# Attention's SBUF arithmetic on another engine, a denser mixing schedule, and a third-batch second layer in products of eighths

## The chip, the cores and the metric

The kernel runs on one core of one Trainium2 chip. The metric is device time in microseconds (us). Engines are named as in the profile: PE (matmul), PEld (PE's weight loads), DVE (vector), ACT (scalar), POOL (GpSimd), SP (the queue that issues every DMA here).

## The reference, cut to what matters

Everything is float32, on x of 4 batches by 2048 tokens by 512 features. A local attention (16 heads of 32, windows of 128 tokens, each window looking at itself and its two neighbours) stands between two layer norms; then comes a feed-forward part whose weights are blended anew for each batch:

```python
x = x + layernorm(attention(layernorm(x), w_qkv))
xn = layernorm(x)
h = relu(xn @ gate_w1.T + gate_b1)
g = mean over tokens of (h @ gate_w2.T + gate_b2)      # 8 numbers per batch
mW1 = W1 + sum_e g[e] * TW1[e]                         # 2048 x 512
mW2 = W2 + sum_e g[e] * TW2[e]                         # 512 x 2048
u = gelu(xn @ mW1.T + mb1)
out = x + layernorm(u @ mW2.T + mb2)
```

## The kernel before, in words

Work is laid out by hand: each engine executes its instructions in the order in which the program text issues them (`manual_schedule`), so a line's place in the text is its place in its engine's queue. There are two stages.

**Attention.** 256 slots, `i = 0..255` (loop at L962): slot `i` is window `i // 4` and head group `i % 4`. In a slot PE computes the scores of slot `i + 1` (L649), turns the probabilities of slot `i` (L686), does up to eight matmuls of "dense" work (products of the QKV projection or of the gate, L518) and the values (L707). DVE takes the row maxima of the next slot's scores (L658), ACT the exponentials (L671) and the copies of the turned probabilities (L691). Lists named `mid`, `rest`, `late` and so on hold what is done at certain points of a slot. `residual` (L326) and `normed` (L334) finish a window after its output: normalise, add the input, store the sum to DRAM, take its statistics, normalise again; the result is turned by PE (`xn2_transposes`, L338) one slot after `normed`. `norm_tile` (L435) normalises an input tile. The dense products follow the Strassen-Winograd scheme of seven products of quarter matrices; `right_factors` (L474) makes the sums T1 to T4 of the right operand, two operations in each of two slots. All of that arithmetic is on DVE. POOL does only the tiny steps of the statistics (L96, L98).

**Blending.** `mixer()` (L106) is a generator. A step loads one expert's 512 KB piece and adds it, scaled, to an accumulator on DVE (L155); after eight experts four quarter sums follow (L163 to L166) and the piece is stored to DRAM in the form that the seven products need. 512 experts in all. `MIXED` (L961) says how many steps each of 16 slots takes: 22 in 16, from slot 85 on; the four quarter sums count as a step. The rest is done in the feed-forward stage by `mixing(...)` between products. Loads run three steps ahead, in four buffers.

**Feed forward.** 16 blocks of 512 tokens (`for K in range(NBK)`, L1485), four blocks to a batch. A block has a first layer (four sets of seven products, L1023, with one `step()` after the other in `middle`) and a second layer. For blocks 0 to 11 that is `second` (L1157): seven products of quarter matrices, each of 16 matmuls of 128x256. For the last batch, blocks 12 to 15, it is `second_deep` (L1237): each of the seven products (index `o`) is again done as seven (`inner(0)` to `inner(6)`, L1308, four matmuls of 128x128 each), so 49 small products. Its right-hand sums are made on DVE as it goes (`inner_sums`, L1233), the results are added on DVE (L1270, by `add` and `emit`), and its weights need a further set of sums, made beforehand by `inner_mixer` (L174): 14 steps of load, four DVE additions and store. Before, that runs in block 11's second layer and block 12's first. At `o == 2` four POOL operations (L1344) turn T1 into T4, which the last product (`o == 6`) reads. At `o == 6` the statistics of two output rows are taken (L1354) before the addition that follows `inner(4)`.

Of the kernel before, what the change touches and what calls it, by code (L numbers as in the profile page):

```python
# [9 lines left out]
F32 = mybir.dt.float32  # L10
# [6 lines left out]
P = 128  # L17
# [17 lines left out]
def sandwich(ctx: ExitStack, tc: tile.TileContext, x, w_qkv, gw1, gb1, gw2, gb2, w1, b1, w2, b2, tw1, tb1, tw2, tb2, out):  # L35
# [44 lines left out]
    DEEP = (NB - 1,)  # L80
# [20 lines left out]
    def normalize(dst, src, sm):  # L101
        mv, rs = sm
        nc.vector.tensor_scalar(dst, src, mv[:, 0:1], rs, ALU.subtract, ALU.mult)


    def mixer():  # L106

        todo = [(b, s, c, e) for b in range(NB) for s in range(2) for c in range(HC) for e in range(NX)]
# [6 lines left out]
        def load(n):  # L115
            b, s, c, e = todo[n]
# [31 lines left out]
        for n, (b, s, c, e) in enumerate(todo):  # L148
# [4 lines left out]
            late = []  # L153
            acc = accs[b, s, c]
            nc.vector.scalar_tensor_tensor(acc, ets.pop(n), g_all[b][:, e : e + 1], acc, ALU.mult, ALU.add)  # L155
            yield
            if e == NX - 1:
# [5 lines left out]
                nc.vector.tensor_tensor(sums[:, 0, :], a21, a22, ALU.add)  # L163
                nc.vector.tensor_tensor(a21, a11, a21, ALU.subtract)
                nc.vector.tensor_tensor(sums[:, 1, :], sums[:, 0, :], a11, ALU.subtract)
                nc.vector.tensor_tensor(sums[:, 2, :], a12, sums[:, 1, :], ALU.subtract)  # L166
                late.append(lambda b=b, s=s, c=c, acc=acc, sums=sums: store(b, s, c, acc, sums))
                yield
        for f in late:
            f()  # L170

    issued = {b: 0 for b in DEEP}

    def inner_mixer(b):  # L174

        todo = [(o, h) for o in order_deep for h in range(2)]
        loaded, late = {}, []

        def load(n):
            o, h = todo[n]  # L180
            two = slice(2 * h, 2 * h + 2)
            et = mix.tile([P, 4, 2, P], F32, tag="exps", bufs=4, name=f"inner_{b}_{o}_{h}")
            nc.sync.dma_start(et[:, :2], m3_d[b][:, o, 0:8:7, two, :])
            nc.sync.dma_start(et[:, 2:], m3_d[b][:, o, 3:7:3, two, :])
            loaded[n] = et

        def store(n, et):
            o, h = todo[n]
            two = slice(2 * h, 2 * h + 2)
            nc.sync.dma_start(m3_d[b][:, o, 1, two, :], et[:, 3])  # L190
            nc.sync.dma_start(m3_d[b][:, o, 2, two, :], et[:, 0])
            nc.sync.dma_start(m3_d[b][:, o, 4:6, two, :], et[:, 1:3])
            issued[b] = n + 1

        for n in range(2):
            load(n)
        yield
        for n in range(len(todo)):
            for f in late:
                f()  # L200
            if n + 2 < len(todo):
                load(n + 2)
            et = loaded.pop(n)
            f11, f21, f12, f22 = (et[:, i] for i in range(4))
            nc.vector.tensor_tensor(f22, f21, f22, ALU.add)
            nc.vector.tensor_tensor(f21, f11, f21, ALU.subtract)
            nc.vector.tensor_tensor(f11, f22, f11, ALU.subtract)
            nc.vector.tensor_tensor(f12, f12, f11, ALU.subtract)
            late = [lambda n=n, et=et: store(n, et)]
            yield  # L210
        for f in late:
            f()
# [48 lines left out]
    def gate_end(b, hsum, bank, spare):  # L261
# [24 lines left out]

        def first_biases():
# [38 lines left out]
    def residual(W_):  # L326
        st = win[W_]
        x1 = st["x1"]
        normalize(x1, st["a"], st["sb"])
        nc.vector.tensor_tensor(x1, x1, st["x"], ALU.add)  # L330
        nc.sync.dma_start(x1_d[W_], x1)
        st["sc"] = stats(x1, f"c{W_}")

    def normed(W_):  # L334
        st = win[W_]
        normalize(st["xn2"], st["x1"], st["sc"])
# [1268 lines left out]
```

## Time and profile before

| what | value |
|---|---|
| median of 3 runs | 3224.7 us (3222.76 to 3225.04) |
| the profiled execution, its own time | 3224.83 us |
| its span, first to last instruction | 3223.0 us |
| granted PE clock | 0.998 |
| PE busy | 3197.1 us (99%) |
| DVE busy | 2278.8 us (71%) |
| ACT busy | 1576.5 us (49%) |
| POOL busy | 676.5 us (21%) |
| attention stage | 0 to about 1674 us |
| blending in the attention stage | from about 589 us |
| feed forward | about 1674 us to the end |

The span is 1.8 us shorter than the time of the same execution. A matmul in float32 stands in the profile as two records, so a product of 16 matmuls is counted x32. A "wait" is idle time of an engine that ended with another's signal. A timeline's first two columns are the start and the duration in us.

### The profile page before, as it was taken

To read this page: it belongs to the slowest core of one execution; us is meant where nothing else is said; L and a number is where in the kernel's file an instruction comes from. 1 tells how busy PE (TensorE), PEld (TensorE's weight loads), DVE (VectorE), ACT (ScalarE), POOL (GpSimd) and SP (SyncE) were. 2 spreads that over 40 slices of the span, in tenths; PEclk is the share of its full clock that TensorE was granted. 3 is DMA by queue.
4 is the path that set the end of the run, shared out by engine and by line. 5 is a ranking of instruction groups with operands and counts; after the bars stand their busy time and mean duration, and the time that the engine had idled before them with its cause. 6 is when DMAs were issued, how large, how long until landed. Compare 5 with 4: busy or idle time off the path is not lost.

```text
span 3223.0 us, 61653 instructions
## 1 busy us (share of the span) xinstructions
PE 3197.1 (99%) x23862; PEld 2697.0 (84%) x23862; DVE 2278.8 (71%) x3307; ACT 1576.5 (49%) x4332; POOL 676.5 (21%) x847
## 2 busy tenths in 40 slices
PE   9999999999999999999999999999999999999998
PEld 7788888888788888878768888888888888889998
DVE  5766666888998889888865665677657667554555
ACT  3777777777777777777761222112222112222222
POOL 0111111111111111110112322323322323332233
PEclk9999999999999999999999999999999999999999
DMA  2111112455555556554677889999899999874555
GB/s 87 54 57 54 40 60 80 138 189 163 193 193 168 178 177 200 194 174 151 211 277 277 310 309 345 355 337 330 311 330 361 341 326 322 305 246 155 193 187 170
DMA packets 363334, 688.88 MB, mean 214 GB/s; under 512 B 27161, under 2 KB 115353, under 8 KB 357026
## 3 DMA queue, kind: packets, MB, share of 16 engines
q1 hardware_dynamic: 363042, 684.94, 61.4%
q8 instruction: 189, 3.10, 0.4%
q14 instruction: 103, 0.84, 0.1%
HBM read 567.39 MB, written 117.44 MB: 212 GB/s over the span
## 4 chain that ended last, share of the span: by engine, by line
PE 94%; DVE 2%; DMA 2%; ACT 1%; POOL 0%; issue 0%; SPq 0%; POOLq 0%; DVEq 0%; ACTq 0%
PE pm L518 23%; PE px L1023 13%; PE ptp L686 11%; PE px L1143 7%; PE sc L649 7%; PE pz L1023 6%; PE po L707 5%; PE pz L1143 5%; PE py L1023 3%; PE py L1143 3%; PE px L1308 2%; PE py2b L1143 2%; PE pz L1308 1%; PE pm L582 1%; PE ptx L340 1%; PE pto L311 1%
## 5 line engine op out<-in xcount | busy, mean ns | idle before, releaser
L155 DVE SCALAR_TENSOR_TENSOR acc<-exps,g,acc 128x1024 f32<-128x1024 f32 x512 | 697.1, 1362 | 66.1 <-DMA exps<-in_tw 60.1
L658 DVE TENSOR_REDUCE nm<-sc 128x2 f32<-128x768 f32 (+1 forms) x512 | 449.2, 918 | 206.8 <-PE sc L649 201.8
L671 ACT ACTIVATE pr<-sc,nm 128x384 f32<-128x384 f32 (+1 forms) x1024 | 572.8, 592 | 11.3 <-DVE nm L658 11.1
L691 ACT COPY prT<-ptp 128x512 f32<-128x512 f32 x732 | 382.9, 595 | 281.3 <-PE ptp L686 281.1
L686 PEld LDWEIGHTS ptp<-ident,pr 128*128 128x128 f32 x2944 | 318.0, 141 | 102.3 <-issue 89.8
L686 PE MATMUL ptp<-ident,pr 128*128 128x128 f32 x2944 | 378.7, 278 | 0.0
L1060 ACT COPY py<-px 128x512 f32<-128x512 f32 x63 | 36.0, 571 | 662.6 <-PE px L1023 662.4
L1023 PE MATMUL px<-tT,w 128*128 128x256 f32 x1512 | 350.1, 379 | 0.6 <-DVE cpv L1083 0.6
L1023 PEld LDWEIGHTS px<-tT,w 128*128 128x128 f32 x1512 | 286.9, 190 | 40.0 <-DVE cpv L1083 1.0
L649 PE MATMUL sc<-k,q 32*128 32x384 f32 (+2 forms) x2816 | 243.2, 423 | 3.7 <-ACT pr L671 3.5
L671 ACT ACTIVATION_READ_ACCUMULATOR pr<-sc,nm 128x1 f32 x1024 | 236.5, 231 | 0.0
L1080 DVE TENSOR_TENSOR cpb<-pz,cpb 128x512 f32<-128x512 f32 x63 | 43.4, 689 | 268.8 <-PE pz L1023 240.1
L96 POOL TENSOR_SCALAR ve_b<-mv_b 128x1 f32<-128x1 f32 x64 | 42.8, 669 | 819.2 <-DVE mv_b L94 819.2
L707 PEld LDWEIGHTS po<-prT,v 128*32 128x32 f32 x5888 | 152.2, 110 | 50.9 <-ACT pr L671 25.4
L707 PE MATMUL po<-prT,v 128*32 128x128 f32 x5888 | 189.7, 275 | 0.2
L649 PEld LDWEIGHTS sc<-k,q 32*128 32x128 f32 x2816 | 118.7, 184 | 74.4 <-issue 53.9
L1143 PE MATMUL px<-w2s,u 128*128 128x256 f32 x784 | 175.1, 379 | 0.0
L518 PE MATMUL pm<-xnT,wqkv 128*128 128x256 f32 x720 | 172.2, 382 | 0.0
L1105 POOL TENSOR_TENSOR t<-u 128x512 f32<-128x512 f32 x60 | 79.9, 1332 | 434.8 <-ACT u L1035 434.8
L1143 PEld LDWEIGHTS px<-w2s,u 128*128 128x128 f32 x784 | 149.0, 190 | 20.2
L518 PEld LDWEIGHTS pm<-xnT,wqkv 128*128 128x128 f32 x720 | 132.0, 190 | 16.7
L1074 ACT COPY cpb<-px 128x512 f32<-128x512 f32 x63 | 36.9, 585 | 182.0 <-PE px L1023 182.0
(295 smaller groups left out, 5911.6 us busy)
## 6 DMA issues: line engine op xcount, KB each, us to landing
exps<-in_tw SPq DMA_DIRECT2D x512, 512.0 KB, 6.0
w2s<-m2d SPq DMA_DIRECT2D x168, 512.0 KB, 8.1
w2s<-m3d SPq DMA_DIRECT2D x84, 512.0 KB, 4.7
acc<-in_w SPq DMA_DIRECT2D x64, 512.0 KB, 6.1
x<-in_x SPq DMA_DIRECT2D x64, 256.0 KB, 4.2
m1d<-acc SPq DMA_DIRECT2D x64, 256.0 KB, 6.3
w<-m1d SPq DMA_DIRECT2D x16, 1024.0 KB, 7.9
fxT<-xTd SPq DMA_DIRECT2D x16, 1024.0 KB, 8.5
```

The source lines that it names most:

```text
L155: nc.vector.scalar_tensor_tensor(acc, ets.pop(n), g_all[b][:, e : e + 1], acc, ALU.mult, ALU.add)
L518: nc.tensor.matmul(bank[u not in chain][:, half, :], lhsT=a[:, kc, ts(half, P)], rhs=b[:, kc, :], start=(u not in (2, 3, 4) and half == kc ...
L649: nc.tensor.matmul(scs[r // 2][:, r % 2, col : col + nj * W], lhsT=q[rows, g, ts(W_ % WB, W)], rhs=k_of[kb][rows, g, j0 * W : (j0 + nj) * ...
L658: nc.vector.tensor_reduce(st["nm"][:, h : h + 2], scs[u][:, :, : nk * W], AX.X, ALU.max, negate=True)
L671: nc.scalar.activation(pr[:, : nk * W], scs[r // 2][:, r % 2, : nk * W], AF.Exp, bias=st["nm"][:, h : h + 1], accum_out=st["den"][:, h : h ...
L686: nc.tensor.transpose(pt[:, r, :], st["pr"][g * 4 + r][:, ts(j, W)], ident)
L691: nc.scalar.copy(prT, pt)
L707: nc.tensor.matmul(po[r * E : (r + 1) * E, n, :], lhsT=v_of[kb][:, jj, h * E : (h + 1) * E], rhs=prT[:, r, :], start=(j == 0), stop=(j == ...
L1023: nc.tensor.matmul(bank[:, f, :], lhsT=factor[:, f, kc * P : (kc + 1) * P], rhs=right[:, kc, :], start=(start and f == 0 and kc == 0), sto ...
L1105: nc.gpsimd.tensor_tensor(t1s[c], b12, us[c][:, :, :Q], ALU.subtract)
L1143: nc.tensor.matmul(bank[:, t, :], lhsT=right(c - c % 2)[:, c % 2, ts(t, P)], rhs=w[:, c % (HC // 2), :], start=(start and c == 0 and t == ...
L1308: nc.tensor.matmul(bank, lhsT=right(p), rhs=w[:, p, :], start=(start and p == 0), stop=True, skip_group_check=True,)
```

## The change

- In the attention loop the arithmetic that reads and writes SBUF alone moves from DVE to POOL: `residual`'s normalise and add, `normed`, `norm_tile` from the third block on, `right_factors` from the second block on, and the blending's four quarter sums (which are then no step of their own). The last window, in the feed-forward stage, and the prologue keep DVE.
- `residual` is split. Its store to DRAM and its statistics become `residual_stats`, at the end of the slot.
- `MIXED` goes from 22 steps in 16 slots to 29; the third step of a slot stands after the first reading of the dense product.
- Batch 2 is added to the batches whose second layer is done in 49 small products. The 14 inner weight sums of batch 2 are put between the steps of batch 3's blending, one after each piece but the first; those of batch 3 now run as the only steps of block 8's first layer. By then all blending is done.
- In `second_deep` the four POOL operations of T4 are issued as two at `o == 3` and two at `o == 4`, and at `o == 6` the addition after `inner(4)` (with the next of the waiting DVE sums) comes before the row statistics, not after them.

```diff
-    DEEP = (NB - 1,)
+    DEEP = (NB - 2, NB - 1)
...
-    def normalize(dst, src, sm):
+    def normalize(dst, src, sm, engine=nc.vector):
         mv, rs = sm
-        nc.vector.tensor_scalar(dst, src, mv[:, 0:1], rs, ALU.subtract, ALU.mult)
+        engine.tensor_scalar(dst, src, mv[:, 0:1], rs, ALU.subtract, ALU.mult)
...
-        todo = [(b, s, c, e) for b in range(NB) for s in range(2) for c in range(HC) for e in range(NX)]
+        todo = []
+        for b in range(NB):
+            again = [(b - 1, o, h) for o in order_deep for h in range(2)] if b - 1 in DEEP else []
+            for s in range(2):
+                for c in range(HC):
+                    todo += [(b, s, c, e) for e in range(NX)]
+                    if s or c:
+                        todo += again[:1]
+                        del again[:1]
...
+            if len(what) == 3:
+                et = ets.pop(n)
+                sum_inner(et)
+                late.append(lambda what=what, et=et: store_inner(*what, et))
+                yield
+                continue
...
-                nc.vector.tensor_tensor(sums[:, 0, :], a21, a22, ALU.add)
+                engine = nc.gpsimd if attending[0] else nc.vector
+                engine.tensor_tensor(sums[:, 0, :], a21, a22, ALU.add)
...
-    def residual(W_):
+    def residual(W_, engine=nc.gpsimd):
         st = win[W_]
         x1 = st["x1"]
-        normalize(x1, st["a"], st["sb"])
-        nc.vector.tensor_tensor(x1, x1, st["x"], ALU.add)
-        nc.sync.dma_start(x1_d[W_], x1)
-        st["sc"] = stats(x1, f"c{W_}")
+        normalize(x1, st["a"], st["sb"], engine)
+        engine.tensor_tensor(x1, x1, st["x"], ALU.add)
+
+    def residual_stats(W_):
+        st = win[W_]
+        nc.sync.dma_start(x1_d[W_], st["x1"])
+        st["sc"] = stats(st["x1"], f"c{W_}")
...
-        def right_factors(K, part, i=0):
+        def right_factors(K, part, i=0, engine=nc.gpsimd):
...
             rest[i + 1].append(lambda W_=W_: residual(W_))
+            late[i + 1].append(lambda W_=W_: residual_stats(W_))
             rest[i + 2].append(lambda W_=W_: normed(W_))
...
-        MIXED = (1, 0, 1, 1, 2, 1, 1, 2, 2, 1, 1, 1, 2, 1, 2, 2)
+        MIXED = (2, 1, 1, 3, 2, 1, 1, 3, 2, 1, 1, 3, 2, 2, 1, 3)
...
-                if o == 2:
-                    for p in range(PAIRS2):
+                if o in (3, 4):
+                    for p in range(2 * o - 6, 2 * o - 4):
                         nc.gpsimd.tensor_tensor(t1[:, p], bottom[:, p, :, :Q], t2[p // 2][:, p % 2], ALU.subtract)
...
+                inner(4, X, summed(2))
+                add(r[1, 1], X, r[1, 1])
+                run(dve, 1)
                 if o == 6:
                     row1 = [stats(y[1][:, t, :], f"d{K}_{t + 2}") for t in range(2)]
...
-                inner(4, X, summed(2))
-                add(r[1, 1], X, r[1, 1])
-                run(dve, 1)
...
-                if K // NBLK in DEEP and k == 0:
+                if b == DEEP[0] and k == 0:
+                    if c == 0:
+                        assert next(blend, 0) == 0
+                        inner = inner_mixer(NB - 1)
                     step = lambda: next(inner, None)
```

## The prediction

> **What bounds the kernel now.** I read first the page's busy times and the chain of work that ended last:
>
> ```profile
> PE 3197.1 (99%) x23862; PEld 2697.0 (84%) x23862; DVE 2278.8 (71%) x3307; ACT 1576.5 (49%) x4332; POOL 676.5 (21%) x847
> ...
> PE 94%; DVE 2%; DMA 2%; ACT 1%; POOL 0%; issue 0%; SPq 0%; POOLq 0%; DVEq 0%; ACTq 0%
> ```
>
> PE is the path. Only three things move the end: less PE work, PE waits that go, PE waits that come. The second view is busy time by stage, for 16 attention slots with blending and 16 without:
>
> ```profile
> 638.96:742.83 103.87, 103.87 (x1041) 84.62 (x1042) 92.08 (x132) 77.33 (x224) 13.54 (x24) 1.00 0.56 186
> ...
> 229.38:333.25 103.87, 103.87 (x1041) 84.62 (x1042) 66.44 (x105) 77.31 (x224) 11.61 (x24) 1.00 0.17 53
> ```
>
> The columns are length, PE, PEld, DVE, ACT, POOL, clock, DMA share, GB/s. DVE goes from 66 to 92 of 103.87 us and PE takes the same 103.87 us. So the attention stage has nothing to win from a lighter DVE, and the list of PE's waits agrees: between 540 and 1100 us it is empty.
>
> The third view is PE's timeline in a block of batch 3 (block 13), at the end of product 2 and of product 6:
>
> ```profile
> 2996.73 1.06 PE L1308 MATMUL pz<-w2s,u 128*128 128x128 f32 x8
> 2998.61 1.16 PE L1308 MATMUL px<-w2s,inner_right 128*128 128x128 f32 x8 [0.82 <-DVE y L1270]
> ...
> 3022.83 1.06 PE L1308 MATMUL pz<-w2s,t 128*128 128x128 f32 x8
> 3024.27 1.16 PE L1308 MATMUL px<-w2s,inner_right 128*128 128x128 f32 x8 [0.39 <-DVE y L1270]
> 3025.26 1.89 PE L1023 MATMUL px<-fxT,w 128*128 128x256 f32 x8
> ```
>
> Small products follow each other every 0.893 us, but these starts lie 1.88 and 1.44 us apart: 0.98 and 0.55 us lost. Both wait for a DVE addition (the one after `inner(4)`), so the fourth view is DVE and POOL there:
>
> ```profile
> 2991.85 1.47 DVE L1233 TENSOR_TENSOR inner_right<-u,inner_right 128x512 f32<-128x512 f32 x1
> ...
> 2996.80 1.55 DVE L1233 TENSOR_TENSOR inner_right<-u,inner_right 128x512 f32<-128x512 f32 x1
> 2998.27 0.28 DVE L1270 TENSOR_TENSOR y<-px,y 128x128 f32<-128x128 f32 x1
> ...
> 3009.84 0.68 DVE L1233 TENSOR_TENSOR inner_right<-u,inner_right 128x512 f32<-128x512 f32 x1
> ...
> 3022.34 0.69 DVE L92 BATCH_NORM_STATS2 st_d<-y 128x6 f32<-128x512 f32 x1
> ...
> 3023.95 0.26 DVE L1270 TENSOR_TENSOR y<-px,y 128x128 f32<-128x128 f32 x1
> ```
> ```profile
> 2990.94 6.86 POOL L1344 TENSOR_TENSOR t<-u,t 128x512 f32<-128x512 f32 x4 [6.14 <-PE pz L1308]
> ```
>
> In product 2, DVE's sums take 1.47 and 1.55 us in place of 0.68 while POOL makes T4, and the addition comes late. In product 6 the two statistics (1.6 us) stand ahead of the addition.
>
> **The second layer of blocks 8 to 11.** Blocks begin at 2739.48 and 2836.17 us (block 11, seven products): 96.69 us. Blocks 13 and 14 begin at 2931.25 and 3025.26, and 15 at 3119.27: 94.01 us each. The difference is 2.68 us, times four blocks: **-10.7 us**. The working agrees: 7 x 6.907 = 48.35 us of PE becomes 49 x 0.893 = 43.76, 4.59 less, of which 1.53 goes back in the two waits and about 0.4 in the hand-overs between the layers. The added POOL, ACT and DVE work of these blocks is what blocks 13 and 14 carry within their 94.01 us; blending is gone from there by then, so DVE's busy time falls from 68 us (block 9) to the 46 of block 13, and the DMA share from 0.92 to 0.49.
>
> **The addition before the statistics.** PE's fifth small product ends at about 3022.8, so the addition can start at about 3023.0 and be done before PE needs it at 3023.7. The 0.55 us go in blocks 8 to 14: 7 x 0.55 = **-3.85 us**. Later on DVE are then the statistics, by 0.9 us; nothing on PE waits for those. In block 15 the end is DVE's own chain, from 3209.69: there the addition must wait some 0.7 us for PE with nothing ahead of it, so the statistics and all after them shift: **+0.7 us**.
>
> **T4 summed later.** The four POOL operations wait for PE to have read T1 in product 1 (the row above says so: released by PE's `pz`, at 2990.94 us). POOL has no other work between there and product 5, so an issue further down the text starts at the same moment and meets the same DVE sums. **0 us**; bounds 0 and -0.98 x 8 = -7.8 us, if something of products 3 and 4 did hold it.
>
> **Entry into block 8.** Block 12, the first deep one before, took 2836.17 to 2931.25 = 95.08 us, 1.07 more than 13: its right-hand sums started 0.3 us later and met POOL twice (the chain shows `inner_right` there). Block 8 gets this too; block 12 keeps it. Besides, all 14 inner sums now stand in block 8's first layer, 16 steps in 48 us, 3.0 us each: a step has 1.7 us of DVE and hangs on a store and a load of about 5 us each (DMA table: 4.8 and 4.9 to landing) with two steps ahead; going round four buffers that is (1.7 + 5 + 5) / 4 = 2.9 us. It just fits. A late step holds the additions behind it on DVE, and PE waits for those. Between 0 and 6 us; I take **+2**.
>
> **Attention: DVE.** Per 16 slots DVE loses 12 normalises of 0.54, 4 adds of 0.69, 8 right sums of 0.69 and about 2.4 sets of four quarter sums of 0.42: 18.8 us. It gains 29 - 19.6 experts of 1.28 us: 12.0. Less by some 7 us. But POOL gets in its way:
>
> ```profile
> L155 DVE SCALAR_TENSOR_TENSOR acc<-exps,g,acc x512: 1251/1278/2352, 589.0 to 2774.8; 128x1024 f32<-128x1024 f32 x171
> ...
> L163 DVE TENSOR_TENSOR sums<-acc x64: 407/420/1476, 628.1 to 2777.2; 128x256 f32<-128x256 f32 x64
> ```
>
> The maxima, 1.07 us above the medians, are what one POOL operation of 1.27 us (L1105) does to a DVE operation that starts beside it. With POOL busy 45% of the time (below) an expert loses about 0.25 us on average: 7 us per 16 slots, and DVE is back at the 92 of 103.87 us at which PE did not wait.
>
> **Attention: POOL.** Added per 16 slots: 12 additions or right sums of 1.27 us (15.2), 3.6 sets of four quarter sums at about half of that (9.2), 12 normalises. The trace has no 128x512 tensor_scalar on POOL: it lies between the 128x1 one (0.22) and well above; nearest is the 1.27 of the same size with two inputs, which I take (15.2). With 13.5 there already: 53 of 103.87 us, or 41 with the low end. For a 128x512 addition POOL's 1.27 us stands against DVE's 0.69 (L330). The Trainium skill (GPSIMD Engine Reference, Engine selection) advises against elementwise work on this engine for the same reason, about twice as slow with two inputs, and calls one-input work roughly line-rate. By that, as an estimate from DVE's 0.54, the 53 us would be 44; the advice itself speaks against the change, and costs nothing as long as nobody waits.
>
> Who could wait? PE for `normed` (one slot, 6.5 us, between), for T1 and T2 (more than a slot), for T3 (about 3 us to spare behind the statistics); DVE for the sum in `residual_stats`, behind which the next row maxima queue. PE has room: at 822.05 us the last exponential of a slot starts, 0.62 us long, and PE wants it at 824.57, 1.9 us later. In most slots ACT reaches the exponentials about 1 us after the first maxima are done. So maxima may be 2 to 3 us late. The worst slot has right sums, quarter sums and `residual` in a row on POOL, 8 us plus collisions, with about 8 us before DVE asks. **+1 us**; from -2.6 (the waits before, at the stage's end) to +34 (0.2 us in each of the 171 slots).
>
> **Transfers.** The inner sums of batch 2 add 1 MB each in blocks 3 to 7, about three in a block, to some 32 MB (334 GB/s in block 4, share 0.93). In block 4 that is near a share of 1. PE's weights come some 20 us ahead; **+0.5**, 0 to 5.
>
> **Sum.** -10.7 - 3.85 + 0.7 + 2 + 1 + 0.5 = -10.3 us, from the profiled execution's 3224.83 us: **3214.5 us**; that execution is 0.1 us from the median of 3224.7.
>
> **Rivals.**
> *The gain is half eaten.* Block 8's entry costs 5, saturated transfers 3, attention 2, in place of 3.5: 3221 us. For it: 2.9 us of a step's 3.0, a share near 1. Against: DVE waited 60 us for experts before, and PE hardly ever.
> *Slower: the attention loop waits for POOL.* POOL's queue is in order, and `normed` on it waits for the window's store to land (2.2 us); behind it stand quarter and right sums. If maxima come more than about 2.5 us late in an ordinary slot, PE stops each time; at 0.2 us a slot x 171 = 34 us, so 3249 us. It turns the sign from 14 / 171 = 0.08 us a slot. For it: DVE has 0 to 1 us idle a slot. Against: 92 of 103.87 us without a wait.
> *T4 does move.* Then 0.98 us less in up to seven blocks: 3208 us.
>
> **How the numbers follow.** Forecast 0.53, half eaten 0.2, slower 0.2, T4 moves 0.07. A measurement here tells 0.2%, 6.4 us. Forecast and T4 are faster by more; the half-eaten case is mostly within. Faster 0.61, same 0.17, slower 0.22. The range takes in the unknown costs of the first two and of T4: 3207 to 3229.
>
> **What would show it.** Blocks 8 to 11 begin about 93.5 us apart, the first more; no wait before the last small product of product 6, still 0.8 us before that of product 2; T4's POOL group still at the end of product 1; 16 middle slots still 103.87 us. Wrong would be PE waits on `pr`, `ptx` or `pm` between 600 and 1650 us.

## The result and the profile after

The changed kernel takes **3344.0 us** (median of 4 runs, 3338.9 to 3345.7) where the kernel before takes 3224.5 us in the same comparison: the ratio is **1.037 (1.035 to 1.039)**, slower. The prediction of 3214.5 us (3207 to 3229) was wrong by 129.5 us. The profiled execution took 3345.66 us, with a span of 3343.7 us.

The busy times and the chain of work that ended last, from the page of the changed kernel:

```profile
PE 3246.5 (97%) x24534; PEld 2736.4 (82%) x24534; DVE 2193.5 (66%) x3107; ACT 1593.0 (48%) x4376; POOL 1496.1 (45%) x1364
...
PE 76%; DMA 8%; DVE 7%; POOL 5%; issue 2%; ACT 1%; SPq 0%; DVEq 0%; POOLq 0%; ACTq 0%
```

PE's share of the chain fell from 94 to 76%. DVE is busy for less time than before, POOL for more than twice as long, and neither is near full. So the loss is not an engine that ran out of time over the whole; it has to be found stage by stage. The starts of the blocks, read from PE's timeline, give this sum (spans 3223.0 and 3343.7 us):

| stage | before, us | after, us | difference | predicted |
|---|---|---|---|---|
| attention, to the first product of block 0 | 1674.4 | 1767.3 | +92.9 | +1 |
| blocks 0 to 3 and 7 | 484.0 | 485.7 | +1.7 | 0 |
| blocks 4 to 6 | 290.1 | 316.9 | +26.8 | +0.5 |
| block 8 | 97.2 | 105.8 | +8.6 | -1.2 |
| blocks 9 to 11 | 290.5 | 280.8 | -9.7 | -9.7 |
| blocks 12 to 14 | 283.1 | 283.3 | +0.2 | -1.7 |
| block 15 and the tail | 103.7 | 103.9 | +0.2 | +0.7 |

What the change was priced for, blocks 9 to 11, came out to the tenth. Three lines are far off: the attention, blocks 4 to 6 and block 8. Blocks 12 to 14 gained nothing in this execution, where 1.7 us were forecast; in run e14 below, with the same code there, they take 281 us. Busy time by stage (length, PE, PEld, DVE, ACT, POOL, clock, DMA share, GB/s), first for slots 96 to 111 and 128 to 143 of the attention, then for blocks 4, 8 and 9 of the changed kernel:

```profile
656.90:766.90 110.00, 107.69 (x1046) 86.00 (x1043) 94.41 (x109) 77.84 (x223) 76.71 (x64) 1.00 0.70 240
...
870.50:988.20 117.70, 109.89 (x956) 87.12 (x952) 89.44 (x110) 74.28 (x218) 78.50 (x64) 0.94 0.69 231
```
```profile
2155.69:2261.58 105.89, 98.97 (x450) 86.47 (x449) 73.33 (x86) 22.55 (x48) 30.69 (x28) 0.97 0.93 331
```
```profile
2569.90:2675.74 105.84, 95.13 (x618) 87.90 (x616) 76.29 (x151) 25.35 (x59) 27.71 (x27) 0.95 0.88 295
2675.74:2769.10 93.36, 92.77 (x618) 86.55 (x617) 45.71 (x97) 24.96 (x59) 28.08 (x30) 1.00 0.49 172
```

DVE's 94.4 us in 16 slots are close to the 92 that were forecast. The 16 slots took 103.9 us before, without a PE wait, and take 110.0 now. POOL has 76.7 us where 53 were forecast. Why is in its groups (mean duration in ns after the bar):

```profile
L103 POOL TENSOR_SCALAR x<-x,mv_a,rs_a 128x512 f32<-128x512 f32 x56 | 145.7, 2602 | 0.1
L103 POOL TENSOR_SCALAR x<-x,mv_c,rs_c 128x512 f32<-128x512 f32 x63 | 143.3, 2274 | 28.7 <-DMA x1d<-x 21.9 <-PE sc L676 3.7 <-PE pm L545 1.9
L103 POOL TENSOR_SCALAR x<-x,mv_b,rs_b 128x512 f32<-128x512 f32 x63 | 132.9, 2110 | 3.0
```

A normalise takes 2.1 to 2.6 us on POOL, not 1.27, against 0.54 on DVE. One slot shows how this reaches PE. POOL's timeline, then DVE's, then PE's, in the same 20 us:

```profile
866.72 1.27 POOL L514 TENSOR_TENSOR tx_True<-gT,tx_True 128x512 f32<-128x512 f32 x1
867.94 0.73 POOL L226 TENSOR_TENSOR sums<-acc 128x256 f32<-128x256 f32 x1
868.75 1.60 POOL L227 TENSOR_TENSOR acc<-acc 128x256 f32<-128x256 f32 x1
...
871.82 2.08 POOL L103 TENSOR_SCALAR x<-x,mv_b,rs_b 128x512 f32<-128x512 f32 x1
873.98 1.27 POOL L354 TENSOR_TENSOR x<-x,xr 128x512 f32<-128x512 f32 x1
...
880.19 3.05 POOL L103 TENSOR_SCALAR x<-x,mv_c,rs_c 128x512 f32<-128x512 f32 x1 [1.05 <-PE ptp L713]
```
```profile
875.28 0.69 DVE L92 BATCH_NORM_STATS2 st_c<-x 128x6 f32<-128x512 f32 x1 [4.93 <-POOL x L354]
876.01 0.18 DVE L94 BATCH_NORM_AGGREGATE mv_c<-st_c 128x2 f32<-128x6 f32 x1
876.11 1.25 DVE L685 TENSOR_REDUCE nm<-sc 128x2 f32<-128x512 f32 x2
```
```profile
877.94 0.70 PE L676 MATMUL sc<-k,q 32*128 32x256 f32 x4 [1.76 <-ACT pr L698]
878.85 0.70 PE L676 MATMUL sc<-k,q 32*128 32x256 f32 x4 [0.21 <-ACT pr L698]
...
883.29 0.66 PE L367 MATMUL ptx<-ident,x 128*128 128x128 f32 x4 [2.72 <-POOL x L103]
```

POOL does right-hand sums, four quarter sums, the normalise and the residual sum in a row. DVE stands 4.93 us at the statistics of that sum. The row maxima (`nm`) queue behind them, ACT's exponentials wait for the maxima, and PE's next scores wait for the exponentials to free the buffer that they write. Then PE waits again, for the second normalise on POOL (the one that starts at 880.19).

Over the stage (500 to 1770 us), PE's longest waits (total us, times, longest), and the group of the scores on the page of the kernel before and of the changed one (busy us, mean ns):

```profile
PE sc L676 <- ACT pr L698: 17.2, 26, 2.1
PE ptx L367 <- POOL x L103: 16.6, 7, 6.3
PE pm L545 <- POOL tx_True L509: 3.0, 2, 1.7
```
```profile
L649 PE MATMUL sc<-k,q 32*128 32x384 f32 (+2 forms) x2816 | 243.2, 423 | 3.7 <-ACT pr L671 3.5
```
```profile
L676 PE MATMUL sc<-k,q 32*128 32x384 f32 (+2 forms) x2816 | 270.4, 425 | 20.7 <-ACT pr L698 20.1
```

Of the stage's 92.9 us, 38 are idle time of PE (8.5 us before, 46.5 after). Some 26 are work lost to a lower clock: the clock records of the two traces have 54.6 us at half clock in this stage, and 3.4 before. The other 29 stand in PE's busy time, nearly all of them at the scores: these fill 27 us more at the same mean duration, because they no longer run side by side (in the timeline above one half starts at 877.94, the other at 878.85, after a wait of its own).

The two parts of the change in the second layer did what was forecast. From block 9 of the changed kernel, PE at the ends of products 2 and 6, and the group of T4 on POOL:

```profile
2741.53 1.06 PE L1339 MATMUL pz<-w2s,u 128*128 128x128 f32 x8
2743.09 1.16 PE L1339 MATMUL px<-w2s,inner_right 128*128 128x128 f32 x8 [0.51 <-DVE y L1301]
...
2767.32 1.06 PE L1339 MATMUL pz<-w2s,t 128*128 128x128 f32 x8
2768.21 1.06 PE L1339 MATMUL px<-w2s,inner_right 128*128 128x128 f32 x8
```
```profile
2735.43 6.86 POOL L1375 TENSOR_TENSOR t<-u,t 128x512 f32<-128x512 f32 x4 [6.14 <-PE pz L1339]
```

The starts at the end of product 6 are 0.89 us apart: that wait is gone. At the end of product 2 they are still 1.56 us apart, and T4 still begins when PE's `pz` of product 1 releases it.

### The profile page after: what moved, and what is told of

Same layout as the page of the kernel before. It is cut to its first block, busy times and chain, and to the rows that moved or that the text cites. A ratio compares the mean times of both kernels' runs of the same rounds, so it can differ in the third digit from the quotient of the medians.

```text
span 3343.7 us, 63920 instructions
## 1 busy us (share of the span) xinstructions
PE 3246.5 (97%) x24534; PEld 2736.4 (82%) x24534; DVE 2193.5 (66%) x3107; ACT 1593.0 (48%) x4376; POOL 1496.1 (45%) x1364
## 4 chain that ended last, share of the span: by engine, by line
PE 76%; DMA 8%; DVE 7%; POOL 5%; issue 2%; ACT 1%; SPq 0%; DVEq 0%; POOLq 0%; ACTq 0%
PE pm L545 18%; PE px L1054 10%; PE ptp L713 9%; PE sc L676 6%; PE px L1339 5%; PE pz L1054 5%; PE po L734 4%; PE px L1174 4%; DMA exps<-in_tw 4%; PE pz L1174 3%; DVE acc L217 3%; PE py L1054 2%; PE pz L1339 2%; PE py L1174 2%; POOL x L103 2%
## 5 line engine op out<-in xcount | busy, mean ns | idle before, releaser
L217 DVE SCALAR_TENSOR_TENSOR acc<-exps,g,acc 128x1024 f32<-128x1024 f32 x512 | 734.7, 1437 | 130.6 <-DMA exps<-in_tw 124.1
L713 PEld LDWEIGHTS ptp<-ident,pr 128*128 128x128 f32 x2944 | 324.3, 143 | 104.4 <-issue 89.1
L713 PE MATMUL ptp<-ident,pr 128*128 128x128 f32 x2944 | 386.8, 282 | 0.1
L1054 PE MATMUL px<-tT,w 128*128 128x256 f32 x1512 | 358.4, 386 | 28.0 <-DVE cpv L1114 28.0
L1054 PEld LDWEIGHTS px<-tT,w 128*128 128x128 f32 x1512 | 290.5, 193 | 70.9 <-DVE cpv L1114 30.5
L676 PE MATMUL sc<-k,q 32*128 32x384 f32 (+2 forms) x2816 | 270.4, 425 | 20.7 <-ACT pr L698 20.1
L676 PEld LDWEIGHTS sc<-k,q 32*128 32x128 f32 x2816 | 131.4, 185 | 105.7 <-issue 53.0
L1339 PE MATMUL px<-w2s,inner_right 128*128 128x128 f32 x1344 | 178.9, 276 | 8.6 <-DVE y L1301 7.0
L1339 PEld LDWEIGHTS px<-w2s,inner_right 128*128 128x128 f32 x1344 | 163.5, 192 | 11.3 <-DVE y L1301 10.6
L96 POOL TENSOR_SCALAR ve_d<-mv_d 128x1 f32<-128x1 f32 x62 | 15.6, 251 | 327.3 <-DVE mv_d L94 327.3
L103 POOL TENSOR_SCALAR x<-x,mv_c,rs_c 128x512 f32<-128x512 f32 x63 | 143.3, 2274 | 28.7 <-DMA x1d<-x 21.9
```

Of the source, the lines that this page charges most:

```text
L103: engine.tensor_scalar(dst, src, mv[:, 0:1], rs, ALU.subtract, ALU.mult)
L676: nc.tensor.matmul(scs[r // 2][:, r % 2, col : col + nj * W], lhsT=q[rows, g, ts(W_ % WB, W)], rhs=k_of[kb][rows, g, j0 * W : (j0 + nj) * ...
L713: nc.tensor.transpose(pt[:, r, :], st["pr"][g * 4 + r][:, ts(j, W)], ident)
L1054: nc.tensor.matmul(bank[:, f, :], lhsT=factor[:, f, kc * P : (kc + 1) * P], rhs=right[:, kc, :], start=(start and f == 0 and kc == 0), sto ...
L1339: nc.tensor.matmul(bank, lhsT=right(p), rhs=w[:, p, :], start=(start and p == 0), stop=True, skip_group_check=True,)
```

## The experiments

"Begin" is the start of the feed-forward stage in the profiled execution. The times of e1 to e4, e17 and e18 are medians of 2 to 11 executions, the others are of one. The changed kernel, e3, e12 and e14 have the same attention code and begin that stage at 1759 to 1771 us, so differences of 10 us there are not told apart. The numbers e1 to e18 are the heads of the runs' names.

| run | what it is | begin, us | time, us |
|---|---|---|---|
| before | | 1674 | 3224.5 |
| after | | 1767 | 3344.0 |
| e1 | normalises on DVE | 1767 | 3341.6 |
| e2 | POOL work, old rate (22 steps, 19.6 experts) | 1688 | 3238.7 |
| e8 | POOL work, 24 steps in 16 slots | 1702 | 3252.7 |
| e3 | POOL work, 29 steps | 1767 | 3319.0 |
| e16 | 29 steps, all on DVE | 1748 | 3299.0 |
| e4 | before, order of the second layer | 1673 | 3223.2 |
| e5 | after, without most expert loads | 1747 | 3322.8 |
| e6 | after, short accumulations | 1704 | 3278.3 |
| e9 | after, even rate | 1746 | 3322.2 |
| e10 | e9, statistics later | 1789 | 3360.8 |
| e7 | e1, own buffer | 1736 | 3308.0 |
| e13 | e7, even rate | 1701 | 3274.4 |
| e11 | after, without batch 2's inner sums | 1784 | 3335.0 |
| e12 | after, inner loads on ACT's queue | 1759 | 3338.6 |
| e14 | after, batch 3's inner sums spread | 1771 | 3333.7 |
| e15 | e13, inner sums spread | 1698 | 3257.6 |
| e17 | e15, by slot | 1692 | 3242.8 |
| e18 | e17, 31 steps | 1698 | 3250.7 |

**Which part costs: the engine, the rate, or the second layer.** In the first run the three normalises go back to DVE:

```diff
-        normalize(x1, st["a"], st["sb"], engine)
+        normalize(x1, st["a"], st["sb"])
...
-        normalize(st["xn2"], st["x1"], st["sc"], engine)
+        normalize(st["xn2"], st["x1"], st["sc"])
...
-                    rest[i + 1].append(lambda K=K, t=t: norm_tile(K, t, nc.gpsimd))
+                    rest[i + 1].append(lambda K=K, t=t: norm_tile(K, t))
```

> The changed kernel with the three normalises of the attention (129 after the residual and before the transposes, and those of the tiles) back on DVE; additions, right-hand sums and quarter sums stay on POOL, 29 experts in 16 slots stay, the third batch's second layer stays. Theory A (the normalise of 2.1 to 2.6 us on POOL, which I had taken at 1.27, fills POOL to 65-70 of 100 us and makes the scores wait): the feed-forward stage begins near 1680 us again in place of 1767, the time falls by some 85 us to about 3260 us. Theory B (29 experts in 16 slots are too many for DVE, whoever normalises): DVE gets 12 x 0.54 = 6.5 us more per 16 slots, and the stage begins at 1767 or later, the time is 3340 us or more. In both, blocks 4 to 6 and 8 stay near 105 us, since nothing in them is changed.

Theory A fell: 3341.6 us (ratio 1.037, 1.035 to 1.038), begin 1767 us. But the waits changed. From the list of DVE's waits in the attention of this run (total us, times, longest):

```profile
DVE x L103 <- DMA x1d<-x: 40.6, 16, 6.2
```

The normalise after the residual works in place, so it waits until the store of x1 has read the buffer; on POOL that wait (21.9 us) had been POOL's, on DVE it holds the maxima. The next two put the POOL edits of the change alone onto the kernel before, first at its old rate, then (e3) with the change's list and the third step of a slot at its later place:

```diff
-        MIXED = (1, 0, 1, 1, 2, 1, 1, 2, 2, 1, 1, 1, 2, 1, 2, 2)
+        MIXED = (2, 1, 1, 3, 2, 1, 1, 3, 2, 1, 1, 3, 2, 2, 1, 3)
```

> The kernel before with the attention's normalises, additions, right-hand sums and quarter sums on POOL, at the old rate of blending (some 20 experts in 16 slots), second layers as before. Theory A (POOL's own length, with the normalises at 2.1 us, holds the scores): POOL is still at 55-60 of 100 us, and the attention stage is 30 to 60 us longer: 3255 to 3285 us. Theory B (the rate): DVE is lighter than before by some 19 us in 16 slots and POOL's delays are taken up by that: the stage is within 5 us of 1674 us, the time within 3220 to 3232 us.

> As the run at the old rate, but with 29 experts in 16 slots, placed as in the changed kernel; second layers as in the kernel before (batch 3 alone in eighths). The attention stage is then that of the changed kernel, and the feed-forward stage that of the kernel before with blending ended earlier. Both theories: it begins at 1767 us, and the time is 3224 + 93 = 3317 us. If blocks 4 to 6 are slow because of the inner sums of batch 2 (transfers), they take 96.7 us here; if they are slow because of something the attention leaves behind, they take 105 us and the time is 3344 us.

At the old rate the ratio is 1.0046 (1.0031 to 1.0061), 14 us, between the two forecasts; at the new one 95 us, as forecast, with blocks 4 to 6 at 96.8, 96.7 and 97.0 us. So the attention's 93 us come with the rate, and the slow blocks with the third batch's second layer. A rate between, on the same kernel:

```diff
-        MIXED = (2, 1, 1, 3, 2, 1, 1, 3, 2, 1, 1, 3, 2, 2, 1, 3)
+        MIXED = (2, 1, 1, 2, 1, 1, 1, 2, 2, 1, 1, 2, 2, 2, 1, 2)
```

> All attention work on POOL as in the changed kernel, second layers as before, 25 experts in 16 slots instead of 20 (3238.7 us, stage begin 1688) or 29 (3319.0 us, 1767). If the loss grows in proportion to the rate: 1688 + 79 x 5/9 = 1732 us, 3280 us. If it is a threshold, where DVE's room is used up: within 10 us of 1690, some 3245 us.

(Its list adds up to 24 steps, not 25.) Begin is 1702 us, 16 middle slots take 104.4 us: a threshold, nearly, not a proportion. And the change's list of 29 on the kernel before, without any POOL edit:

> The kernel before with 29 experts in 16 slots and nothing else: all of the attention's work stays on DVE, second layers as before. DVE's work in 16 slots is then 92 + 12 us of accumulations + 1.6 us of quarter sums = 106 us against PE's 103.87. If moving work to POOL was what cost (its length, its collisions): the stage begins earlier than in the changed kernel, 1674 + 10.7 x 2 to 4 us = 1695 to 1720 us. If POOL did help and the rate alone is to blame: 1767 us or later. Feed-forward blocks as in the kernel before, 96.7 us.

Begin is 1748 us, between the two forecasts. This separates the two parts: the rate costs 74 us when DVE does everything, and the move to POOL, which was to pay for the rate, adds 19 (11 to 23 over the four runs of that attention code).

**What holds DVE at that rate.** Two runs that leave work out, by the loads and by the arithmetic:

```diff
+            if attending[0] and e > 1:
+                ets[n] = ets_kept[e % 2]
+                return
```
```diff
+            if attending[0]:
+                et, part = et[:, :, :16], acc[:, :, :16]
+            nc.vector.scalar_tensor_tensor(part, et, g_all[b][:, e : e + 1], part, ALU.mult, ALU.add)
```

> The changed kernel in which, during the attention, 14 of the 16 experts of each sum are not loaded (DVE adds the first two again instead): every accumulation of 1.28 us stays, most of the transfers that SP issues for them go. Leaves out: the blended weights of the first batches are then other numbers. Theory D (SP's one queue: an expert's load stands behind stores that wait for POOL, experts come late, and DVE stands): the feed-forward stage begins near 1690 us in place of 1767, as at the old rate. Theory B (DVE itself: 29 accumulations of 1.28 us leave no room for waits on POOL and on PE): it begins at 1745 us or later.

> The changed kernel in which, during the attention, each accumulation covers 32 columns of a partition instead of 1024: all transfers and waits stay, DVE loses some 1.1 us x 29 = 32 us of work in 16 slots. Leaves out: most of the blending of the first batches. Theory D: the loads are issued in the same order and the stage stays near 1767 us, above 1740 in any case. Theory B: the stage begins at 1675 to 1695 us.

Without the loads 20 us of the 93 go, with short accumulations 63 (and with them most of the time in which they can meet POOL's work). So DVE's own time is most of it; late experts are a part. But is it its amount, or its place? The even rate keeps the amount:

```diff
+        MIXED = (2, 2, 1, 2, 2, 2, 1, 2, 2, 2, 1, 2, 2, 2, 2, 2)
```

> The changed kernel with the same 29 experts in 16 slots, but never three in a slot: the third of slots 3, 7 and 11 goes to the slots 1, 5 and 9, that of slot 15 to slot 14 and one of slot 13 stays. In the changed kernel the stretch of DVE that holds three accumulations and two row statistics takes 7.9 us busy and 1.4 idle against PE's 6.5 us a slot, while the stretch before it stands idle for 2 us. Theory burst (the place of the work in its slot): the stage begins at 1700 to 1720 us in place of 1767. Theory room (DVE has none on average): 1750 us or later.

```diff
-            late[i + 1].append(lambda W_=W_: residual_stats(W_))
+            rest[i + 2].append(lambda W_=W_: residual_stats(W_))
```

> The even rate of the run before, and besides the statistics of x1 (DVE) stand one slot later, just ahead of the normalise that needs them, where POOL's sum has long been made: DVE's wait for POOL's sum (27.9 us in 20 waits in the changed kernel) goes. If that wait, where it stands, is what uses up DVE's room: the stage begins 20 to 30 us earlier than with the even rate alone. If something else on DVE takes its place: within 8 us of it.

The even rate gave 21 us, less than half of what the theory of place asked. Taking the statistics later took DVE's wait for POOL's sum away (25.9 us in 18 waits became 2.5 in 3) and cost 43 us: PE's waits for the second normalise went from 28.9 to 58.4 us, because on POOL it then starts too late for its transposes. With the normalises on DVE there is no such chain:

```diff
-                **dict.fromkeys(("a", "x1", "xn2"), work.tile([P, D], F32, tag="x1", name=f"x1_{W_}")),
+                **dict.fromkeys(("a", "x1"), work.tile([P, D], F32, tag="x1", name=f"x1_{W_}")),
...
+            win[W_] |= dict.fromkeys(("x", "xn2"), load_tile(W_ // WB, W_ % WB, "xr", 2))
```

> The run with the normalises on DVE, and besides the normalise ahead of the transposes writes into the residual input's buffer instead of in place, so it no longer waits for the store of x1 to have been read (40.6 us in 16 waits on DVE in that run); the load of the residual input moves two slots later to have the buffer free. If that wait is what holds DVE: the stage begins near 1767 - 60 = 1707 us, or earlier. If DVE has no room in any case (theory B): 1750 us or later, with the wait replaced by others.

And the same with the even list above:

> Normalises on DVE into a buffer of their own (that run: stage begin 1736, 3308 us) with the even rate (never three experts in a slot). If the two gains add up (30 us from the buffer, 20 us from the even rate): the stage begins near 1716 us, 3288 us in all. If both gains were the same room on DVE: 1730 to 1736 us.

1736 us lies between the two forecasts of e7; 1701 us is better than that of e13: the gains do add, and the second, 35 us, is larger than forecast. These are 16 middle slots (from slot 96) of the run with everything on DVE, of the even rate with normalises on POOL, and of the last run:

```profile
650.20:761.90 111.70, 108.49 (x1044) 86.78 (x1040) 106.39 (x150) 78.03 (x223) 13.50 (x25) 1.00 0.70 232
```
```profile
654.40:764.60 110.20, 104.72 (x1044) 84.62 (x1040) 92.12 (x110) 78.27 (x223) 76.24 (x64) 1.00 0.70 237
```
```profile
652.60:756.60 104.00, 104.00 (x1047) 84.61 (x1043) 97.85 (x122) 77.62 (x223) 49.01 (x50) 1.00 0.74 251
```

In the first DVE is full: 106.4 us of work for 103.9 of PE's. In the second it is busy for 92.1 us and PE waits; in the third it is busy for 97.9 of 104.0 and PE does not wait at all in these slots, at the same 29 steps. So the theory that DVE lacks room on average holds for e16 and falls for the changed kernel. The lists of waits from 500 to 1780 us tell what went, first of the second run, then of the third:

```profile
PE ptx L367 <- POOL x L103: 28.9, 18, 6.6
DVE st_c L92 <- POOL x L354: 25.9, 18, 4.9
```
```profile
PE sc L675 <- ACT pr L697: 7.0, 10, 1.9
DVE st_c L92 <- POOL x L354: 4.6, 3, 2.1
```

PE no longer waits for a normalise on POOL, and DVE hardly for POOL's sum. So what costs in the changed kernel is where the work stands: DVE and PE stand still for POOL, and three accumulations of 1.45 us follow in the slot after such a wait. How much each of these costs by itself is not shown.

**Blocks 4 to 6 and block 8.**

```diff
             if len(what) == 3:
-                et = ets.pop(n)
-                sum_inner(et)
-                late.append(lambda what=what, et=et: store_inner(*what, et))
                 yield
```

> The changed kernel with the inner sums of the third batch as empty steps: their loads (7 MB), additions and stores (7 MB) in blocks 3 to 7 are left out, so that batch's second layer computes with zeros in their place (they are written once, early in the attention). If the transfers of blocks 4 to 6 are over what the queue moves (35 MB in 105 us, 331 GB/s, where the kernel before moved 334 GB/s): these blocks take 96.7 us, 27 us less in all. If they are slow because of DVE (additions ahead of PE's): 96.7 as well, but then DVE's waits for experts in these blocks, 52 us in the changed kernel, stay. Block 8 keeps its 105 us, since its sums are those of the last batch.

```diff
-        nc.sync.dma_start(et[:, :2], m3_d[b][:, o, 0:8:7, two, :])
+        nc.scalar.dma_start(et[:, :2], m3_d[b][:, o, 0:8:7, two, :])
```

> The changed kernel with the loads of the inner sums issued from ACT's queue instead of SP's. In block 8 SP's queue stands for PE to free the weight buffers (36 us in 28 waits in that block) and inner loads stand behind it. If that is why they come late: block 8 takes 96 to 98 us in place of 105.8, and blocks 4 to 6 stay near 105 if they are bound by what the queues can move, or fall too if theirs is the same wait. If block 8 is bound by the latency of a step itself (2.9 us against 3.0, my estimate) nothing changes: 105 us.

```diff
-                if b == DEEP[0] and k == 0:
+                if b == DEEP[0] and k < 3:
                     if c == 0:
                         assert next(blend, 0) == 0
-                        inner = inner_mixer(NB - 1)
-                    step = lambda: next(inner, None)
+                        inner = inner_mixer(NB - 1, slice(5 * k, 5 * k + 5))
+                    turns = iter((1, 0, 1, 0))
+                    step = lambda: next(turns) and next(inner, None)
```

> The changed kernel with the inner sums of the last batch done five each in the first layers of blocks 8 and 9 and four in block 10, in place of all 14 in block 8. Theory transfers (block 8's first layer moves 14 MB of inner sums beside 13 MB of weights; the queue's share is 0.99 in its first half): block 8 takes 94 to 97 us in place of 105.8, blocks 9 and 10 up to 1 us more than their 93.5. Theory latency of a step (load, sum, store in turn): with twice the time between steps it goes as well, but then the share in block 8 before was not the cause; the row to read is DVE's wait for the inner loads, 14 us in six waits in the changed kernel, the longest 5.1 us at a share near 1. If block 8 is slow for what it is the first block in eighths (its right-hand sums): it stays above 100 us.

Without the inner sums blocks 4 to 6 take 96.7 us each (the run's attention is 16 us longer, with the 14 stores of zeros in it). With the loads on ACT's queue block 8 got worse, 112.1 us, which neither forecast had. DVE's waits for the inner loads stayed (13.7 us in five, in place of 14.1 in six), so SP's order was not what made these late; PE stood 8.5 us for ACT besides. Blocks 4 to 6 took 309.9 us together there, in place of 316.9. With the sums spread over three blocks, block 8 took 94.8 us, and blocks 9 and 10 stayed at 93.4. Block 4 without inner sums, and block 8 with a third of them:

```profile
2173.39:2270.08 96.69, 96.69 (x449) 85.12 (x448) 64.08 (x73) 22.56 (x48) 28.72 (x27) 1.00 0.89 322
```
```profile
2571.63:2666.40 94.77, 93.03 (x617) 86.62 (x616) 55.98 (x115) 24.97 (x59) 26.97 (x27) 1.00 0.68 227
```

The sign that e11's forecast named is DVE's wait for experts in blocks 4 to 6, in the changed kernel and in e11:

```profile
DVE acc L217 <- DMA exps<-in_tw: 52.0, 26, 6.2
```
```profile
DVE acc L220 <- DMA exps<-in_tw: 17.7, 14, 2.7
```

It fell by two thirds, which speaks for the transfers. But e11 leaves out DVE's additions with the bytes, so it does not wholly part the two. Nor does e14 part the bytes of block 8's first layer from the latency of its steps, since it halves the rate of both. In the changed kernel's block 8 the inner loads and stores landed after 4.5 and 3.4 us (medians), sooner than the 5 and 5 of the prediction, so the usual step is not slower than it was priced; DVE still stood 14.1 us for six late ones.

A late transfer does its harm by way of DVE's order, as the best of the later runs shows in its block 4:

```profile
2120.29 1.28 DVE L217 SCALAR_TENSOR_TENSOR acc<-exps,g,acc 128x1024 f32<-128x1024 f32 x1 [4.50 <-DMA exps<-in_tw]
2121.49 1.29 DVE L1452 TENSOR_TENSOR fx<-fx,y 128x512 f32<-128x512 f32 x2
2122.69 5.70 DVE L217 SCALAR_TENSOR_TENSOR acc<-exps,g,acc 128x1024 f32<-128x1024 f32 x3
...
2131.48 0.68 DVE L1118 TENSOR_TENSOR cpv<-px,cpv 128x512 f32<-128x512 f32 x1
```

One expert is 4.5 us late. Two output additions, three more experts, one sum of the first layer's products (`cpb`) and four quarter sums stand behind it and ahead of the next such sum, `cpv`, for which PE waits 4.1 us.

**The second layer's order alone.** Of the change's diff only the hunk of T4 and those of the addition at `o == 6`, on the kernel before:

> The kernel before with the two moves in the second layer alone (addition ahead of the statistics in the last column, T4 in two halves later), which act on blocks 12 to 15 only. By the prediction's steps: 0.55 us less in three blocks, 0.7 us more in block 15's tail, T4 nothing: 3223.5 us. If T4's move also takes the wait at the end of product 2: 0.98 us less in four blocks besides, 3219.5 us. If both do nothing: 3224.5 us. The place to read is the distance of the small products' starts at the ends of products 2 and 6 (1.88 and 1.44 us before, 0.89 without a wait).

3223.2 us, ratio 0.9999 (0.9990 to 1.0008): no difference. In the profiled execution blocks 12 to 14 are each shorter by 0.6 us, as forecast, and block 15 by 0.4 up to PE's last product, but the stretch after that product grows from 9.4 to 11.5 us: in the last block the statistics wait for the addition. The forecast 0.7 us there was 1.7 net. Part of it is a late load: a product just ahead of that addition waits 0.69 us for its weights. In the changed kernel, with the same order and without that wait, block 15 and the tail are 0.2 us longer.

**Towards a version that wins.** e15 is e13 with the edit of e14. e17 places the steps by slot and takes some from blocks 4 to 6 to block 0; e18 has 31 steps (`i % 16`, and slots 133 and 247 thinned too):

```diff
+        THIN = (128, 129, 130, 131, 193, 194, 195, 242, 243, 244)
+        MIXED = {i: 1 if i in THIN or i % 8 == 2 else 2 for i in range(85, NS)}
...
+                elif K == 0:
+                    step = mixing(1, 1, 1, 1)
...
+                more = {4: (1, 2, 1, 2, 1, 2, 1), 5: (2, 3, 2, 2, 2, 3, 2), 6: (2, 3, 2, 2, 2, 3, 2)}.get(K, (3, 2, 3, 2, 2, 3, 2))
```

> Both: normalises on DVE into their own buffer, even rate, and the last batch's inner sums spread over blocks 8 to 10. If the parts add: the time of the run with buffer and even rate less 9 to 11 us, 3278 us if that one gives 3288. Still above the kernel before by some 50 us: 40 from the attention, 25 from blocks 4 to 6, 15 gained in blocks 8 to 14.

> The combined run (normalises on DVE in their own buffer, even rate, last batch's sums spread: 3257.6 us) with the experts placed by slot: one instead of two in the ten slots where that run lost time against the kernel before (128 to 131, 193 to 195, 242 to 244, whose PE work is shorter, 4.8 to 5.8 us), two in most others, and the transfers moved from blocks 4 to 6 (33 to 36 MB each, 340 GB/s) to block 0 (289 GB/s). If loss is where DVE's work in a slot exceeds PE's time in it: the stage begins near 1684 us in place of 1697.7, blocks 4 to 6 take 97 to 103 us: 3228 to 3236 us. If it is the mean rate: the loss moves to other slots, stage 1695 us or later, 3240 us or more.

> As the run by slot, with 31 experts in 16 slots (two in fifteen of them, one in the thin ones) and so fewer in blocks 4 to 7 (29 to 34 MB). If DVE still has room in the middle slots (where 29 at an even rate cost 0.13 us in 16 slots): the stage begins within 5 us of the run by slot, and blocks 4 to 6 are 97 to 100 us: 3222 to 3230 us, beside the kernel before. If 31 is over DVE's room (66 + 31 x 1.28 + 8 = 114 less 12 us on POOL = 102 of 103.87 us): each 16 slots lose 2 us or more, stage 1705 us or later, 3240 us or more.

The first came out 17 us under e13, better than its forecast. The other two missed what the theory of place asked (3228 to 3236 and 3222 to 3230 us). Their times are those of the other theory, 3240 us or more, but they begin earlier than it asked (1692 and 1698 us, against 1695 and 1705). The best of the three is e17 with 3242.8 us, ratio 1.006 (1.004 to 1.008), still slower than before. Its sum: +18 us in the attention, +14 in blocks 4 to 6, -15 in blocks 8 to 14. Of its thinned slots, 128 to 131 lose 1 us in place of 6 in e15, but 193 and 194 lose 5.5, and the stretch after slot 240 another 6: place is a part, not all. With more steps the middle slots lose again: 16 of them take 104.9 us at e17's 30 steps and 109.2 at 31, with DVE at 99.2, which fits a DVE without room there. No version that ran beats the kernel before.

## Why the prediction was wrong

- *What bounds the kernel*: right. PE is the path, and the losses are PE's waits and what follows them.
- *Second layer, -2.68 and -0.55 us a block*: right, blocks 9 to 11 fell by 3.3, 3.4 and 3.0 us. *T4, nothing*: right, it starts at the same release in both orders. *Block 15's tail, +0.7*: right in sign; +0.2 in the changed kernel, 1.7 in the run with the order alone.
- *Attention: DVE*, "DVE is back at the 92 of 103.87 us at which PE did not wait": **this step failed**. The size was right (94.4 us; by luck in part, since an accumulation lost 0.17 us beside POOL, not 0.25, with POOL busy for longer than forecast) and the inference wrong. Priced at +1 with the steps on POOL, the stage took +92.9. A busy share at which PE did not wait holds for that arrangement of the work; DVE works in order, and 92.1 us with waits on POOL went with 6 us more per 16 slots, while 97.9 without them cost none.
- *Attention: POOL*, 1.27 us for a normalise: measured 2.1 to 2.6, of which nearest row and bounds ("well above" 0.22) gave no warning; 77 us of POOL in place of 53. The Trainium skill (GPSIMD Engine Reference, Engine selection) calls one-input work roughly line-rate; here the one-input normalise with two scalars a partition ran 3.9 times as long as on DVE (2.1 to 0.54), and the two-input addition 1.9 times (1.27 to 0.68), so its advice against elementwise work held and its exception did not.
- *The worst slot has "8 us plus collisions, with about 8 us before DVE asks", +1*: the slot was named rightly, and it is the one in the timelines above. Zero slack was priced at 1 us. The rival built on it (0.2 us a slot, 34 us, chance 0.2) had the mechanism of the late maxima; the loss was 0.54 us a slot, and POOL alone was not its cause (14 us in e2 at the old rate; the rate on DVE alone costs 74 of the 93).
- *Transfers, +0.5*: measured +26.8. The bytes were foreseen, about three MB on top of some 32, and priced at next to nothing because PE's weights come 20 us ahead. At the 334 GB/s that I had read off, 3 MB need 9 us; blocks 4 to 6 grew by 9.2, 8.1 and 9.5 us, and block 4 moved 35.1 MB (331 GB/s for 105.9 us). The lead of PE's weights did not help, because PE waits for DVE there (18.2 us in four waits), behind late experts.
- *Entry into block 8, +2, "It just fits"*: measured +12.5 over block 9. The usual step fits, and some steps come late; whether for the bytes or for the latency of a step is not shown.
- *The rivals*: T4 did not move. The slower rival, the attention loop waiting for POOL, came nearest: the waits on `pr`, `ptx` and `pm` that were to show the prediction wrong are PE's list in that stage (17.2, 16.6 and 3.0 us). They are some 37 of the 93 us; the lower clock and the scores that no longer run side by side are the rest.

What stays open: what makes a step of block 8 late, how blocks 4 and 6 of e17 still lose 6 us each with fewer experts in them (bytes, or DVE's order behind one late expert), and the 6 to 10 us after slot 240 that e15 and e17 still lose.

## What to carry to other kernels

Before work moves to an idle engine, follow each result to its reader, slot by slot, and only then add up busy time: where the reader's queue is in order, as here, all that stands behind the reader waits too. A busy share without waits is no allowance; look at the fullest slot and at what stands behind each wait. Where a stage's transfers already run at 0.92 of the share, price added bytes at the rate of that stage, and place them where the share is low.

## What the hardware showed

A PE wait costs more than its length. Busy time by stage around a wait of 1.5 us that ended at 907.00 us in the changed kernel (the clock is the third number from the right):

```profile
900.00:910.00 10.00, 8.27 (x50) 5.20 (x43) 6.46 (x10) 4.29 (x12) 7.07 (x8) 0.90 0.72 224
910.00:920.00 10.00, 10.00 (x90) 8.44 (x89) 8.25 (x9) 6.96 (x19) 4.05 (x2) 0.76 0.63 185
920.00:930.00 10.00, 10.00 (x84) 8.05 (x86) 7.70 (x10) 6.66 (x21) 7.88 (x7) 1.00 0.72 263
```

PE's granted clock was 0.90 and 0.76 in these first 20 us, together 3.4 us of work. In slots 128 to 143 PE stood 7.8 us and its busy time grew by 10.5, from 99.4 to 109.9 us; the mean clock of 0.94 makes about 7 of these. The Trainium skill (TensorE: Matmul & The Clock Gate, Why this matters for your kernels) asks for no gaps above about 3 us; here one of 1.5 us was followed by a lower clock. The length of a wait does not decide it alone: after the 1.76 us that ended at 877.94 the clock stayed at 1.00 up to 884 us.

DVE and POOL slow each other: an accumulation takes 1.28 us on average with all work on DVE at 29 steps and 1.45 us in the changed kernel, and a normalise on POOL took 2.08 us at 871.82, while DVE stood, and 3.05 at 880.19, beside three accumulations.
